# A graph layer on one core: more gathered rows moved to the sync engine and ScalarE, layers spread over three blocks, counts and merges on VectorE

## The chip, the core and the metric

The kernel runs on one core of a Trainium2 chip. The metric is device time in microseconds, the median of several runs. The core has TensorE (PE in the profile: matrix products, weights loaded by PEld), VectorE (DVE), ScalarE (ACT), GpSimd (POOL) and the sync engine (SP). DMAs are issued by SP, ScalarE and GpSimd.

## What is computed

There are 12,500 nodes with 128 features in `x`, and 200,000 edges from `src` to `dst`, sorted by `dst`. The reference, cut to what matters:

```
h    = max(layernorm(x), 0)                  # 12500 x 128
agg  = segment_sum(h[src], dst) / max(deg, 1)
h0   = relu(agg @ Wg + h @ Ws + bg)          # 128 wide
h1   = tanh(h0 @ W1 + b1)                    # 512 wide
h2   = tanh(h1 @ W2 + b2)                    # 512 wide
out  = x + h2 @ W3 + b3                      # 128 wide
```

`deg` counts the edges of each `dst`.

## The kernel before, in words

**Edges.** The 200,000 edges are cut into 1563 chunks of 128. For a chunk, 128 rows of `h` (512 bytes each) must be fetched, one for each `src`, into a 128 x 128 tile. A one-hot matrix of 128 edges by a window of nodes (144 in most chunks, since `dst` is sorted) says to which node each edge belongs. One product of TensorE with the rows as weights (`add`, L432) adds the chunk's rows into the sums of a block of nodes. There are 28 blocks, 23 of 512 nodes and smaller ones at the end.

**Where rows come from.** First the layer norm is computed and written to a table in HBM (`htab`, L173 to L246). Most chunks fetch their rows with one indirect DMA on GpSimd (`gather`, L308). The tiles of these are a ring of `AHEAD` = 32 buffers, so the gather of a chunk can be issued when the chunk 32 places earlier has been added. 80 "raw" chunks (256 to 655, 8 of each 40) are gathered straight from `x` while the table is still being made (L149) and normed on VectorE (`centre`, `raw_scaled`), with the squares on ScalarE. 38 "slow" chunks use no gather: each of their 128 rows is one plain DMA of 512 bytes whose address is read into a register. SP issues them for 23 chunks (tile `srows`), ScalarE for 15 (tile `arows`), in `row_loads` (L337). `SLOW0`, `EACH` and `EACH_A` choose these chunks: one on SP after each 58 gathered chunks, one on ScalarE after each 76. `row_loads` is a generator; the main loop resumes it at a pace that loads a chunk while `EACH` (or `EACH_A`) gathered chunks go by. 32 row addresses are read by one register load before their 32 DMAs. SP's generator stops after each 32 rows, ScalarE's after each 4. `rows_one` has two buffers for each of the two names.

**Order on the queues.** PE, ACT and SP instructions of the main part are kept in program order each (`pe`, `act`, `sp_dma`). On SP the row loads share the queue with three large DMAs for each block: own rows of `htab` (`hb`, L480, one buffer, issued 52 chunks and turned 10 chunks before its block begins), rows of `x` (`xb`), and the store of the output. On ScalarE they share it with the activations of the layers. Each DMA of SP and ScalarE signals its landing on one of eight semaphores, handed out in turn over both queues in the order in which the scheduler places the DMAs. A DMA that takes a semaphore waits until the semaphore's last DMA has landed, whichever of the two engines issued that one.

**Counts.** For each group of 8 chunks VectorE makes the one-hot matrices (`onehot`, L374, four buffers) and sums them over the chunks (`cnt`). `count` (L404) adds these on TensorE by products with a matrix of ones, some ten for each block, and takes the reciprocal on VectorE (`rd`).

**Edges of blocks.** A chunk whose window reaches two blocks goes to an extra sum (`edge`), which ScalarE copies to SBUF (`sums`, two buffers). `merge` (L463) adds it to both blocks by products with the identity. `part0` then multiplies by `rd` (L533).

**Layers.** `layers` (L599) gives the steps of a block: `part0` (h0), `part1` (h1), `part2` (h2), `part3` and `part4` (output, turned back by TensorE, residual added). A block takes the last two parts of the block before between its own, so layers of two blocks overlap. One step is taken for every second chunk until chunk `QUICK` = 1376. After that a plan of expected landing times in the loop (L669) places the steps.

Of the kernel before, what the change touches and what calls it, by code (L numbers as in the profile page):

```python
# [22 lines left out]
F32 = mybir.dt.float32  # L23
BF16 = mybir.dt.bfloat16
# [7 lines left out]
P = 128  # L32
# [7 lines left out]
STEP = 40  # L40
AHEAD = 32
SLOW0 = 120
EACH = 58
EACH_A = 76
TOGETHER = 4
LOADS = 32
LATE = 12
LEAD = 10
QUICK = 1376

# [10 lines left out]
def windowed(ctx, tc, x, src, dst, Wg, Ws, bg, W1, b1, W2, b2, W3, b3, out, flag):  # L61
# [26 lines left out]
    for c in range(SLOW0, NCH - 12):  # L88
        if raw(c):
            continue  # L90
        if ns <= 0:
            slow_s.append(c)
            ns = EACH
        elif na <= 0 and c < QUICK:
            slow_a.append(c)
            na = EACH_A
        else:
            ns -= 1
            na -= 1
# [22 lines left out]
    raws = ctx.enter_context(tc.tile_pool(name="raws", bufs=1))  # L122
    rows_one = ctx.enter_context(tc.tile_pool(name="rows_one", bufs=2))
    rows_in = ctx.enter_context(tc.tile_pool(name="rows_in", bufs=AHEAD))
# [56 lines left out]

    def centre(pool, xt, k, stats):
        nc.vector.tensor_reduce(stats[:, 0], xt, AX.X, ALU.add)
        nc.vector.scalar_tensor_tensor(xt, spread(stats[:, 0], k), -1.0 / D, xt, op0=ALU.mult, op1=ALU.add)
        sq = pool.tile([P, k, D], F32, name=f"sq{k}")
        nc.scalar.activation(sq, xt, AF.Square)
        nc.vector.tensor_reduce(stats[:, 1], sq, AX.X, ALU.add)
# [114 lines left out]
    def flat(t):  # L302
        return t.rearrange("p a b -> p (a b)")

    def sp_dma(*a):
        tc.keep_in_program_order(nc.sync.dma_start(*a))  # L306

# [17 lines left out]
    class act:  # L325
# [8 lines left out]
        def dma(*a):  # L334
            tc.keep_in_program_order(nc.scalar.dma_start(*a))  # L335

# [32 lines left out]
    for t in oh_bufs:  # L369
        nc.vector.memset(t, 0.0)  # L370

    counts = {}

    def onehot(g):  # L374
        k = min(GRP, NCH - g * GRP)
        lo, w = window(g * GRP)
        is_raw = raw(g * GRP)
        oh = ed.tile([P, GRP, W_RAW], F32, name="ohr", bufs=2) if is_raw else oh_bufs[g % OHS]
        if not is_raw and w < oh_w[g % OHS]:
            nc.vector.memset(oh[:, :, w : oh_w[g % OHS]], 0.0)  # L380
            oh_w[g % OHS] = w
        nc.vector.tensor_tensor(  # L382
            oh[:, :k, :w], lane[:, None, :w].to_broadcast([P, k, w]),
            dloc[:, g * GRP : g * GRP + k][:, :, None].to_broadcast([P, k, w]), op=ALU.is_equal,
        )
        ohs[g] = oh
        step, n = (oh.shape[2], w) if is_raw else (PITCH - per, w + per * (k - 1))
        cnt = ed.tile([P, PITCH], BF16, name="cnt", bufs=16)
        part, row, col = oh.ap
        shifted = bass.AP(tensor=oh.tensor, offset=oh.offset, ap=[part, [col[0], n], [step * col[0], k]])  # L390
        with nc.allow_low_precision(reason="whole numbers up to the chunks of a group"):
            nc.vector.tensor_reduce(cnt[:, :n], shifted, AX.X, ALU.add)  # L392
        counts[g] = (lo, n, cnt)

# [9 lines left out]
    def count(b):  # L404

        n, m = blocks[b]
        dg = flat(ps_m.tile([P, 4, P], F32, name="pm"))
        groups = sorted({c // GRP for c in reach[b]})
        for g in groups:
            lo, w, cnt = counts[g]  # L410
            a0, a1 = max(lo, n), min(lo + w, n + m)
            pe.matmul(
                dg[:, a0 - n : a1 - n], ones, cnt[:, a0 - lo : a1 - lo], start=(g == groups[0]), stop=(g == groups[-1]),
                skip_group_check=True,
            )
        rd = ml.tile([P, BLK], F32, name="rd", bufs=3)
        nc.vector.tensor_scalar(rd[:, :m], dg[:, :m], 1.0, None, op0=ALU.max)  # L417
        nc.vector.tensor_reduce(total[:, b : b + 1], dg[:1, :m], AX.X, ALU.add)
        nc.vector.reciprocal(rd[:, :m], rd[:, :m])  # L419
        rds[b] = rd  # L420
# [11 lines left out]
    def add(c):  # L432
# [4 lines left out]
        if c in across[b]:  # L437
# [7 lines left out]
            if c == across[b][-1]:  # L445
                sums = ed.tile([P, BLK], F32, name="sums", bufs=2)
                act.copy(sums[:, : e1 - e0], edge.pop(b)[:, : e1 - e0])
                edges[b] = sums
# [5 lines left out]
        else:  # L454
            start = False
        pe.matmul(
            acc[b][:, a0 - n : a1 - n], rows, oh[:, a0 - lo : a1 - lo], start=start,
            stop=(c == inside[b][-1] and not across[b]), skip_group_check=True,
        )

    edges = {}

    def merge(b):  # L463

        e0, e1 = edge_span(b)
        sums = edges.pop(b)
        for i in (b, b + 1):
            n, m = blocks[i]
            a0, a1 = max(e0, n), min(e1, n + m)
            new = i not in acc  # L470
            if new:
                acc[i] = ps_a.tile([P, BLK], F32, name="agg")
            pe.matmul(
                acc[i][:, a0 - n : a1 - n], ident, sums[:, a0 - e0 : a1 - e0], start=new, stop=(i == b),
                skip_group_check=True,
            )

    owns, hTs, xss, stores = {}, {}, {}, []

    def own(s):  # L480

        n0 = s * BLK
        n = min(BLK, N - n0)
        k = -(-n // P)
        hb = ml.tile([P, BLK // P, D], F32, name="hb", bufs=1)
        sp_dma(hb[:, :k], htab[n0 : n0 + k * P, :].rearrange("(t p) d -> p t d", p=P))
        owns[s] = hb

    def own_turned(s):
# [4 lines left out]
        for t in range(k):  # L494
            pe.transpose(pt[:, t, :], hb[:, t, :], ident)
        hT = ml.tile([P, BLK], F32, name="hT")
        act.copy(hT[:, : k * P], pt[:, :k, :].rearrange("p t n -> p (t n)"))
# [17 lines left out]

    h0s, h1s, h2s, h3s = {}, {}, {}, {}

# [4 lines left out]
    def wide(b):  # L522

        return (P, 2) if blocks[b][1] <= P else (BLK, 1)

    def part0(b):
        n, mm, hop = costs(b)
        s, off = divmod(blocks[b][0], BLK)
        if n == BLK:
            own_part(b)  # L530
        yield 0, 0
        mT = ml.tile([P, BLK], F32, name="mT")
        nc.vector.tensor_tensor(mT[:, :n], acc[b][:, :n], rds.pop(b)[:, :n], op=ALU.mult)  # L533
        yield mm, 0
        p0 = flat(ps_m.tile([P, 4, P], F32, name="pm"))
        pe.matmul(p0[:, :n], ws, hTs[s][:, off : off + n], start=True, stop=False)
        yield mm, n / 90
        pe.matmul(p0[:, :n], wg, mT[:, :n], start=False, stop=True)
        h0s[b] = ml.tile([P, BLK], F32, name="h0")
# [14 lines left out]
    def part2(b):  # L554
        n, mm, hop = costs(b)
        size, bufs = wide(b)
        h1, h2s[b] = h1s.pop(b), ml.tile([P, HM, size], F32, name=f"h2_{size}", bufs=bufs)
        for m in range(HM):
# [39 lines left out]

    def layers(b, before):  # L599


        part = lambda f, *a: lambda: f(*a)
        last = [] if before is None else [part(part3, before), part(part4, before)]
        if reach[b][-1] + LEAD < QUICK:
            return one_by_one(
                part(part0, b), *last[:1], part(part1, b, True), *last[1:], part(part2, b)
            )
        return one_by_one(
            *last, part(part0, b), part(part1, b, False), part(part2, b), part(part3, b), part(part4, b)
        )  # L610

    order = [c for c in range(NCH) if not raw(c) and c not in slow]
    loading = row_loads(slow_s, mybir.EngineType.SP, sp_dma, "srows", LOADS)
    loading_a = row_loads(slow_a, mybir.EngineType.Activation, act.dma, "arows", TOGETHER)
# [21 lines left out]

    own(0)
    own_turned(0)
    onehot(0)
    onehot(1)  # L640
    counted = 0
    for c in range(NCH):
# [3 lines left out]
        if c % GRP == 0 and g + 2 < ngrp:  # L646
# [3 lines left out]
            if 2 <= g < 2 + NRAW:  # L650
                centre(ed, raw_rows[g - 2], GRP, raw_stats(g - 2))
            if g == 2 + NRAW:
                factors(stats_raw)

        while c % GRP == GRP // 2 and counted < len(blocks) and reach[counted][-1] // GRP <= g + 1:
            count(counted)
            counted += 1
# [3 lines left out]
        if not raw(c) and c not in slow:  # L661
            behind += 1
            batch = behind * P // (EACH * LOADS)
            if behind > SLOW0 - 2 * EACH and batch > (behind - 1) * P // (EACH * LOADS):
                next(loading, 0)
# [12 lines left out]
        if done < len(blocks) and (c - lead if across[done] else c) >= reach[done][-1]:  # L678
            if across[done]:
                merge(done)  # L680
            quick = reach[done][-1] + LEAD >= QUICK

            before = done - 1 if done and reach[done - 1][-1] + LEAD < QUICK else None
            work.append([layers(done, before), 0, 0, 0, quick and blocks[done][1] <= P])
            done += 1
        if (c // span + 1) * BLK < N:
            if c % span == span - 52:
                own(c // span + 1)
            if c % span == span - 10:
                own_turned(c // span + 1)  # L690
        if c < QUICK:
# [385 lines left out]
```

## Time and profile before

| what | value |
|---|---|
| median of 3 runs | 1932.92 us (1929.8 to 1933.98) |
| profiled execution: time, span | 1931.2 us, 1928.7 us |
| busy: POOL, PE, DVE, ACT | 1442.0, 1299.0, 1066.8, 228.1 us |
| instructions in it: POOL, PE, DVE, ACT | 1533, 5212, 651, 362 |
| row loads of SP and of ScalarE | 2944 and 1920, 0.5 KB each |
| granted TensorE clock | 0.866 of full speed |
| DMA | 139.69 MB, mean 72 GB/s |

The span runs from the first to the last instruction; 2.5 us of the execution's own time lie outside it. Busy times of different engines overlap. PE counts two records for each float32 product. Issuing a DMA counts as busy on POOL alone, not on SP or ACT; the timeline shows their issues as SPq and ACTq.

### The profile page before, as it was taken

The page shows a single profiled execution, that of the slowest core. Times are in us where ns is not written, and L with a number is a line of the kernel's source. Part 1 is how long each engine was busy: PE and PEld are TensorE (multiplying, and loading weights), DVE is VectorE, ACT ScalarE, POOL GpSimd, SP SyncE. Part 2 cuts the span into 40 slices and gives each one's busy share as a digit, 9 for nine tenths or more (in the row PEclk, how much of TensorE's full clock was granted, in tenths as well). Part 3 has the DMA queues.
Part 4 walks back from the last instruction along what each step waited for, and adds up shares of the span by engine and source line. Part 5 has one row for each costly group of instructions (what it writes and reads, how often), then busy time and mean ns, then how long its engine had stood idle before and what let it go on. Part 6 is the DMA issues. An engine that isn't in the chain of part 4 may idle for free.

```text
span 1928.7 us, 24991 instructions
## 1 busy us (share of the span) xinstructions
PE 1299.0 (67%) x5212; PEld 819.1 (42%) x5212; DVE 1066.8 (55%) x651; ACT 228.1 (12%) x362; POOL 1442.0 (75%) x1533
## 2 busy tenths in 40 slices
PE   0056487775757678758775676566776746878787
PEld 0034354443535445534443344344443424554466
DVE  7964865555556856636544465354554536645430
ACT  1100111010101111111100110001101101101122
POOL 7777777777777777777777777777777777777774
PEclk9999688898878888888887898878988879879698
DMA  8822222222222222222222222222222222222221
GB/s 202 233 65 53 55 67 59 61 71 60 67 71 66 66 70 67 71 71 61 65 61 66 71 61 65 61 71 66 61 66 66 61 70 61 71 78 71 66 62 40
DMA packets 128692, 139.69 MB, mean 72 GB/s; under 512 B 35036, under 2 KB 103294, under 8 KB 128336
## 3 DMA queue, kind: packets, MB, share of 16 engines
q0 software_dynamic: 48800, 100.04, 20.5%
q1 hardware_dynamic: 72654, 33.65, 6.4%
q10 hardware_dynamic: 7076, 4.32, 0.9%
q14 instruction: 119, 0.97, 0.2%
q8 instruction: 43, 0.70, 0.2%
HBM read 125.07 MB, written 12.82 MB: 71 GB/s over the span
## 4 chain that ended last, share of the span: by engine, by line
DMA 31%; PE 28%; issue 17%; SPq 11%; DVE 5%; POOL 3%; ACTq 3%; ACT 1%; POOLq 0%; DVEq 0%
PE pm L297 16%; DMA rows<-htab,scol 16%; SPq L306 10%; PE agg L297 6%; DMA arows<-htab 5%; PE edge L297 4%; DMA srows<-htab 4%; POOL rows L310 3%; DMA hb<-htab 3%; ACTq L335 3%; DVE cnt L392 2%; DMA xt<-in_x_dram 2%; PE pt L300 1%; DVE oh L382 1%; SPq L344 1%
## 5 line engine op out<-in xcount | busy, mean ns | idle before, releaser
L310 POOL DMA_INDIRECT rows<-htab,scol x1445 | 1363.4, 944 | 440.8 <-issue 258.9
L297 PE MATMUL pm<-h,w 128*128 128x512 f32 (+4 forms) x1344 | 649.1, 580 | 26.3 <-ACT h L329 26.3
L297 PE MATMUL agg<-oh,rows 128*128 128x144 f32 (+3 forms) x2068 | 484.4, 342 | 219.9 <-DMA rows<-htab,scol 217.1
L297 PEld LDWEIGHTS agg<-oh,rows 128*128 128x128 f32 x2068 | 360.7, 215 | 530.1 <-DMA rows<-htab,scol 395.2
L382 DVE TENSOR_TENSOR oh<-shared,dloc 128x1152 f32<-128x1152 f32 (+2 forms) x186 | 243.4, 1314 | 605.8 <-PE edge L297 354.9
L392 DVE TENSOR_REDUCE cnt<-oh 128x200 bf16<-128x1600 f32 (+2 forms) x186 | 525.8, 2832 | 5.4
L297 PEld LDWEIGHTS pm<-h,w 128*128 128x128 f32 x1344 | 223.4, 206 | 42.2 <-ACT h L329 29.4
L297 PEld LDWEIGHTS edge<-oh,rows 128*128 128x128 f32 x822 | 150.3, 219 | 160.5 <-issue 85.8
L297 PE MATMUL edge<-oh,rows 128*128 128x144 f32 (+2 forms) x822 | 181.8, 333 | 39.7 <-DMA rows<-htab,scol 39.4
L300 PE MATMUL pt<-ident,hb 128*128 128x128 f32 x98 | 24.5, 398 | 242.7 <-DMA hb<-htab 242.7
L329 ACT ACTIVATE h<-pm,b2c 128x512 f32<-128x512 f32 (+4 forms) x112 | 70.8, 632 | 447.6 <-PE pm L297 229.3
L300 PEld LDWEIGHTS pt<-ident,hb 128*128 128x128 f32 x98 | 16.8, 204 | 246.3 <-issue 246.3
L153 POOL DMA_INDIRECT raw<-in_x_dram,rsrc x80 | 77.7, 971 | 25.4 <-issue 23.8
L329 ACT ACTIVATE h<-pm,b1c 128x512 f32<-128x512 f32 (+4 forms) x112 | 69.9, 632 | 203.2 <-PE pm L297 107.3
L419 DVE RECIPROCAL rd<-rd 128x512 f32<-128x512 f32 (+4 forms) x28 | 81.8, 2920 | 0.0
L332 ACT COPY hT<-pt 128x512 f32<-128x512 f32 (+1 forms) x25 | 14.4, 577 | 410.2 <-PE pt L300 383.9
L589 DVE TENSOR_TENSOR o<-pt,xb 128x512 f32<-128x512 f32 x23 | 15.8, 688 | 75.9 <-PE pt L300 75.9
L417 DVE TENSOR_SCALAR rd<-pm 128x512 f32<-128x512 f32 (+4 forms) x28 | 17.2, 616 | 63.1 <-PE pm L297 63.1
L212 PE MATMUL pm<-ident,idx_f 98*128 98x98 f32 x32 | 6.2, 376 | 62.0 <-DVE idx_f L208 55.7
L297 PE MATMUL pm<-mT,wg 128*128 128x512 f32 (+4 forms) x56 | 32.6, 669 | 22.7 <-DVE mT L533 22.5
L329 ACT ACTIVATE h<-pm,bgc 128x512 f32<-128x512 f32 (+4 forms) x28 | 17.7, 632 | 240.0 <-PE pm L297 144.1
L297 PE MATMUL pm<-hT,ws 128*128 128x512 f32 (+4 forms) x56 | 34.8, 711 | 0.0
(72 smaller groups left out, 496.9 us busy)
## 6 DMA issues: line engine op xcount, KB each, us to landing
srows<-htab SPq DMA_DIRECT2D x2944, 0.5 KB
arows<-htab ACTq DMA_DIRECT2D x1920, 0.5 KB
rows<-htab,scol POOLq DMA_INDIRECT x1445
hb<-htab SPq DMA_DIRECT2D x24, 256.0 KB
xb<-in_x_dram SPq DMA_DIRECT2D x23, 256.0 KB
out_dram<-o SPq DMA_DIRECT2D x23, 256.0 KB
htab<-h SPq DMA_DIRECT2D x6, 896.0 KB
xt<-in_x_dram SPq DMA_DIRECT2D x5, 896.0 KB
```

The source lines that it names most:

```text
L153: nc.gpsimd.indirect_dma_start(out=t[:, j, :], out_offset=None, in_=x, in_offset=bass.IndirectOffsetOnAxis(ap=rsrc[:, g, j : j + 1], axis=0),)
L297: tc.keep_in_program_order(nc.tensor.matmul(*a, **k))
L300: tc.keep_in_program_order(nc.tensor.transpose(*a, **k))
L306: tc.keep_in_program_order(nc.sync.dma_start(*a))
L310: nc.gpsimd.indirect_dma_start(out=r, out_offset=None, in_=htab, in_offset=bass.IndirectOffsetOnAxis(ap=scol[:, c : c + 1], axis=0),)
L329: tc.keep_in_program_order(nc.scalar.activation(*a, **k))
L335: tc.keep_in_program_order(nc.scalar.dma_start(*a))
L344: loads, vs = nc.values_load_multi_w_load_instructions(place[i : i + 1, p0 : p0 + LOADS], engines=[engine], min_val=0, max_val=(N - 1) * ROWB,
L382: nc.vector.tensor_tensor(oh[:, :k, :w], lane[:, None, :w].to_broadcast([P, k, w]), dloc[:, g * GRP : g * GRP + k][:, :, None].to_broadcas ...
L392: nc.vector.tensor_reduce(cnt[:, :n], shifted, AX.X, ALU.add)
L417: nc.vector.tensor_scalar(rd[:, :m], dg[:, :m], 1.0, None, op0=ALU.max)
L419: nc.vector.reciprocal(rd[:, :m], rd[:, :m])
```

## The change

- The constants give 27 slow chunks to SP (one after each 50 gathered chunks) and 20 to ScalarE (one after each 62, now up to chunk 1438). 1436 chunks are gathered, where 1445 were.
- SP's generator stops after each 4 rows instead of 32. `rows_one` has 4 buffers a name, the gathers' ring 44.
- `in_turn` ties each row load, block load and store of SP and ScalarE to the one before it in program order, over both engines, for the scheduler alone: no wait on the chip comes with it. The eight semaphores are so handed out in program order.
- Each group's counts are added on VectorE to a bfloat16 tile of the block (`deg`). One product with ones remains for a block.
- `merged` replaces `merge`: VectorE adds the block's own sums and the one or two edge sums stretch by stretch, and multiplies by `rd`. It is a step of its own (`mean`).
- The squares of the raw chunks move from ScalarE to VectorE.
- Layers: until `QUICK` (now 1312), the steps of a block are its mean, output part 3 of the block two before, its `part0`, `part2` of the block before, `part4` of the block two before, and its `part1`. `LEAD`, the distance at which a block's steps start, is 16 chunks instead of 10.
- `hb` has two buffers; it is loaded half-way through the block two before its own and turned half-way through the block before. `hT` has 3 buffers, `sums` 4 (288 wide).
- `xb` is loaded in `part2` instead of `part0`.

The diff, cut to its core:

```diff
-AHEAD = 32
-SLOW0 = 120
-EACH = 58
-EACH_A = 76
+AHEAD = 44
+SLOW0 = 110
+EACH = 50
+EACH_A = 62
...
-LEAD = 10
-QUICK = 1376
+LEAD = 16
+QUICK = 1312
...
-        elif na <= 0 and c < QUICK:
+        elif na <= 0 and c < NCH - 2 * EACH_A:
...
-    rows_one = ctx.enter_context(tc.tile_pool(name="rows_one", bufs=2))
+    rows_one = ctx.enter_context(tc.tile_pool(name="rows_one", bufs=4))
...
-        sq = pool.tile([P, k, D], F32, name=f"sq{k}")
-        nc.scalar.activation(sq, xt, AF.Square)
+        sq = pool.tile([P, k, D], F32, name=f"sq{k}", bufs=bufs)
+        if bufs > 1:
+            nc.scalar.activation(sq, xt, AF.Square)
+        else:
+            nc.vector.tensor_tensor(sq, xt, xt, op=ALU.mult)
...
+    turn = []
+
+    def in_turn(start):
+
+        tc.keep_in_program_order(start)
+        if turn:
+            tc.add_manual_dep(
+                start.ins, turn.pop(),
+                mybir.DependencyInfo(mybir.DependencyClass.NoSync, mybir.DependencyReason.DATA), reason="in_turn",
+            )
+        turn.append(start.ins.name)
+
     def sp_dma(*a):
-        tc.keep_in_program_order(nc.sync.dma_start(*a))
+        in_turn(nc.sync.dma_start(*a))
...
         def dma(*a):
-            tc.keep_in_program_order(nc.scalar.dma_start(*a))
+            in_turn(nc.scalar.dma_start(*a))
...
-        counts[g] = (lo, n, cnt)
+            for b, (n0, m) in enumerate(blocks):
+                a0, a1 = max(lo, n0), min(lo + n, n0 + m)
+                if a0 < a1:
...
+                    d = counts[b][:, a0 - n0 : a1 - n0]
+                    nc.vector.tensor_tensor(d, d, cnt[:, a0 - lo : a1 - lo], op=ALU.add)
...
+        pe.matmul(dg[:, :m], ones, counts.pop(b)[:, :m], start=True, stop=True)
...
+    def merged(b, mT):
...
+        cuts = sorted({a for a0, a1, _, _ in parts for a in (a0, a1)})
+        for a0, a1 in zip(cuts, cuts[1:]):
+            over = [t[:, a0 - o : a1 - o] for p0, p1, t, o in parts if p0 <= a0 and a1 <= p1]
+            out = mT[:, a0 - n : a1 - n]
+            s = over[0]
+            for t in over[1:]:
+                nc.vector.tensor_tensor(out, s, t, op=ALU.add)
+                s = out
+            nc.vector.tensor_tensor(out, s, rd[:, a0 - n : a1 - n], op=ALU.mult)
...
-        hb = ml.tile([P, BLK // P, D], F32, name="hb", bufs=1)
+        hb = ml.tile([P, BLK // P, D], F32, name="hb", bufs=2)
...
+        if c % span == span // 2 and (c // span + 1) * BLK < N:
+            own_turned(c // span + 1)
+            if (c // span + 2) * BLK < N:
+                own(c // span + 2)
...
-                part(part0, b), *last[:1], part(part1, b, True), *last[1:], part(part2, b)
+                part(mean, b), *of(older, part3), part(part0, b), *of(prev, part2), *of(older, part4),
+                part(part1, b, True),
...
-    loading = row_loads(slow_s, mybir.EngineType.SP, sp_dma, "srows", LOADS)
+    loading = row_loads(slow_s, mybir.EngineType.SP, sp_dma, "srows", TOGETHER)
```

## The prediction

> **What bounds the kernel now.** I read the page's groups first, then POOL's own timeline and its busy time by stretch, then what PE and SP wait for, and last the timeline of SP's queue.
>
> ```profile
> L310 POOL DMA_INDIRECT rows<-htab,scol x1445 | 1363.4, 944 | 440.8 <-issue 258.9
> ```
>
> ```profile
> 88.74 0.94 POOL L153 DMA_INDIRECT raw<-in_x_dram,rsrc  x1 [0.30 <-issue]
> 89.98 0.94 POOL L153 DMA_INDIRECT raw<-in_x_dram,rsrc  x1 [0.30 <-issue]
> ```
>
> ```profile
> 200.00:300.00 100.00, 75.58 (x81) 0.72 0.24 60
> ...
> 1800.00:1900.00 100.00, 75.63 (x81) 0.91 0.23 59
> ```
>
> A gather takes 0.94 us, the next starts 0.30 us later, and every stretch of 100 us from 200 to 1900 holds 80 or 81 of them. The last starts at 1908.0, the first at 105.0: (1908.0 - 105.0) / 1444 = 1.2486 us each, the pitch of two neighbours with nothing waiting between them. POOL never stops, from the raw gathers to the end. The page's 75% is a full engine: the other quarter is the 0.30 us. DMA is at 0.23 to 0.29 of its engines, so bytes don't bind. The end stands 20.7 us behind the last gather (1928.7 - 1908.0): landing, last adds, the last block's layers, its store.
>
> ```profile
> PE pt L300 <- DMA hb<-htab: 242.7, 19, 31.4
> PE agg L297 <- DMA rows<-htab,scol: 217.1, 338, 6.8
> PE pm L297 <- ACT h L329: 26.3, 12, 12.4
> ```
>
> ```profile
> SPq L306 <- DMA arows<-htab: 397.1, 270, 40.0
> ```
>
> PE waits for gathered rows, as it should, and up to 31 us at a time for a block's own rows (`hb`), which queue on SP behind row loads. None of it reaches POOL: the tightest ring buffer came free 3.0 us before its gather (near 600 us, PE's adds set beside the gathers in order). SP waits most for ScalarE's row loads, whose semaphores it shares.
>
> **What the change removes.** Nine gathers: 9 x 1.2486 = 11.2 us, all on the path. Last gather: 105.0 + 1435 x 1.2486 = 1896.8. The start is covered: the nine more address loads sit on ScalarE before and between the last norm pieces; `hb`, which waits for the whole table, issues at 96.6, so 8.4 us are spare before the gather at 105.0.
>
> PE loses the 294 products for counts (23.8 us) and 108 records of merges (21.3 us), and gets 28 wide products (an estimate: 0.4 us each, from 0.27 for 200 columns). Worth nothing at the end, since PE waits 217 us for rows already; it helps PE catch up.
>
> **What it adds on VectorE.** The changed program has 294 count adds, 28 clears, 188 operations in `merged` instead of 28 multiplies, and 10 squares. From 0.25 us (the 128-wide add) for small ones and 1.2 us (a 1024-wide raw operation) for squares: 294 x 0.25 + 28 x 0.2 + 188 x 0.28 - 28 x 0.65 + 12 = 126 us, from 1067 to about 1190, 62% of the span. Tightest are groups 2 to 11, each of 8 x 1.25 = 10 us: 7.9 us now, then 7.9 + 1.2 + 2 x 0.25 = 9.6. One-hots are made two groups ahead, so 20 us cover this. Taken at 0; without that cover PE would start each group late. In the tail the last block's mean takes three operations instead of one: +0.4 us.
>
> Here a rule speaks against the change. The Trainium skill, "SBUF — State Buffer", section "Who interferes with whom", says that a VectorE instruction with two SBUF inputs contends with a GpSimd instruction that reads SBUF, each blocking the other whole, though not with one that only writes. The kernel before keeps one input in PSUM nearly everywhere; count adds, squares and the multiplies by `rd` after a merge now have both in SBUF. The gather names an index column in SBUF, so by the rule some 420 x 0.25 + 12 = 117 us could block gathers, three quarters of it (0.94 of 1.25) on top of one: +88 us. The trace has one such operation:
>
> ```profile
> 89.17 0.23 DVE L261 SCALAR_TENSOR_TENSOR dloc<-rdst,low 128x80 f32<-128x80 int32 x1
> ```
>
> It lies wholly inside the gather of 88.74, which took 0.94 as ever; all 1445 table gathers took 0.940 to 0.961 us. By the row it costs 0. I take the row and keep 88 us as the end of the cost.
>
> **What it moves: the two row-load queues.** SP must load 128 rows in 50 x 1.2486 = 62.4 us instead of 72.4, ScalarE in 77.4 instead of 94.9. In the changed program's order 2407 of SP's 3456 row loads wait for SP's own load four before (650 of 2944 now), 753 for one of ScalarE's (797 now). Such a wait ends 1.5 us after the earlier load's issue, the median by the semaphores' records, so about 0.38 us a row.
>
> ```profile
> 900.40 12.21 SPq L306 DMA_DIRECT2D srows<-htab  x32
> ...
> 958.38 41.50 SPq L306 DMA_DIRECT2D srows<-htab  x64
> 999.98 0.41 SPq L306 DMA_DIRECT2D out_dram<-o  x1
> 1003.24 25.29 SPq L306 DMA_DIRECT2D srows<-htab  x64
> ```
>
> ```profile
> 1642.06 36.43 SPq L306 DMA_DIRECT2D srows<-htab  x96
> ```
>
> The last line is SP alone: (36.43 - 2 x 2.8) / 3 = 10.3 us for 32 rows, 2.8 us being the gap of a register load. Beside ScalarE, 32 rows take 12.2 to 13.1 where nothing else stops them (12.7), and far more where SP waits for ScalarE. Flowing, a chunk needs 4 x 12.7 + 4 x 2.8 + 2.5 large DMAs x 0.45 = 63.1 us, against 62.4: a loss of 0.7 a chunk, 18 us over 26 chunks. A second rule would say worse: "DMA: Bandwidth & Descriptors", section "Anatomy of one DMA", puts a DMA's fixed part at about 2.0 us (for GpSimd's path). With four in flight that is 0.5 us a row, 76 us a chunk, and the loads could not keep up. The measured 1.5 us on these queues decides.
>
> The loss has cover. By the order and the waits of the changed program, the last row of an SP chunk depends on PE only up to 66 or more adds before its use (11 at the tightest now), ScalarE's 28 or more (27 now), and `hb` 66 or more after the start-up (10 now). 66 adds are about 79 us at 1.2 us each. Behind that, the ring of 44 lets PE be 44 x 1.2486 = 55 us late before POOL stops. ScalarE: 16 rows take 6.5 us, so 128 take 52; four register loads at 2.8 and 10 activations at 0.66 make 70 of 77.4 us. Queued behind a late row load on ScalarE are activations, and PE's layer products wait for these with three PSUM tiles of cover; PE waits 26 us for them now. With layers over three blocks most activations have other work between them and their reader. On SP `hb`, `xb` and stores stand behind row loads; only `hb` can hold PE, and its 242.7 us should nearly go. What is late next is again gathered rows. I take 0 for the queues.
>
> **Sum.** 1928.7 - 11.2 + 0.4 = 1917.9 us span; with the 2.5 us around it (1931.2 - 1928.7) 1920.4. The median stood 1.7 above that execution: 1922.1.
>
> **Rivals.**
>
> *The queues become the bound.* ScalarE waits in order for PE, SP for ScalarE's semaphores, and the stalls stay. The two lines from 958 to 1028.5 show 70.2 us for 128 rows. Against 62.4 that is 7.8 lost a chunk, 203 over 26; 79 and 55 are absorbed, 69 are stalled gathers: 1991. It decides from (79 + 55) / 26 = 5.2 us lost, 67.6 us a chunk, and 63.1 is not far below. For it: the 397 us, and ScalarE's lead barely grows. Against it: a good part of that stall is a ring (PE held by `hb`, ScalarE by PE, SP by ScalarE) that the earlier `hb` opens, and eight semaphores in program order let neither queue wait for a load placed later. Chance 0.18.
>
> *VectorE blocks the gathers*, up to 1922 + 88 = 2010, as costed. One overlapping row is thin evidence. Chance 0.05.
>
> *A short stall eats the gain*: PE or ScalarE is once over 55 us late, most likely in the raw part, where PE has 25% more chunks a gather, and 4 to 15 us of gathers are lost: 1926 to 1937. Chance 0.09.
>
> *The change doesn't do what it says*: excluded for counts, since the changed program holds exactly 1436 gathers, 3456 and 2560 row loads, and its landing waits follow program order.
>
> **Chances and range.** The forecast has 0.68, with its own range 1919 to 1927: POOL's chain leaves nothing to gain beyond it, and start and tail may move by a few us. About 0.2% (3.9 us) is what a measurement of this kernel can tell from no change. Faster 0.68, same 0.08 (most of the short stall), slower 0.24 (the queues, VectorE, the rest). The range goes to 1950, which takes in the short stall and mild forms of the queues' case and leaves out some 0.18 above and 0.02 below.
>
> **What would show it.** Right: 1436 gathers at 1.25 us with no gap over 0.31, the last near 1897; `hb` gone from PE's waits; SP's 128 rows under 67 us; VectorE near 1190 us. Wrong: gathers that wait for PE's adds, with PE waiting for `srows`, `arows` or activations (the queues), or gathers longer than 0.96 us (VectorE).

## The result: slower, and the profile after

The changed kernel takes 1981.57 us (1974.13 to 1983.79), the kernel before beside it 1933.45 (1929.8 to 1934.18): a ratio of 1.0246, 95% interval 1.0216 to 1.0276. Forecast was 1922.1. The profiled execution has a span of 1981.9 us, and the gathers themselves are as forecast (the page's groups, columns as before):

```profile
L325 POOL DMA_INDIRECT rows<-htab,scol x1436 | 1364.1, 950 | 488.1 <-issue 247.1
```

There are 1436 of them, the first at 104.1, and POOL's idle time grew from 440.8 to 488.1 us though nine gathers are gone. POOL's busy time by stretch shows where (busy us, gathers, granted clock, DMA share, GB/s):

```profile
200.00:300.00 100.00, 64.77 (x66) 0.67 0.18 46
300.00:400.00 100.00, 72.84 (x77) 0.76 0.23 61
...
1200.00:1300.00 100.00, 75.55 (x81) 0.81 0.24 66
...
1600.00:1700.00 100.00, 59.91 (x64) 0.78 0.24 64
1700.00:1800.00 100.00, 71.62 (x76) 0.80 0.23 62
```

For over 1200 us in the middle POOL is as full as before. The loss lies around 300 and around 1700. Summed over the gathers' starts in the trace: nine gathers less, -11.2 us; an earlier start, -0.9; starts further apart than 1.2486 us, +59.3 (stalls of 18.8 near 300, 4.4 near 690, 20.9 near 1700 and 5.1 near 1790; some 6 of lengthened gathers; some 4 of a pitch of 1.252 instead of 1.249); and a longer tail, +6.1 (the tail is the time behind the last gather: that is at 1955.1, and 26.9 us follow, where 20.7 did). Together 53.3; the spans differ by 53.2.

**The first stall, read backwards.** POOL's timeline, then PE's, then ScalarE's (start, duration, instruction, in brackets the idle time before it and what ended it):

```profile
303.57 0.94 POOL L325 DMA_INDIRECT rows<-htab,scol  x1 [18.97 <-PE agg L300]
```

```profile
275.28 2.08 PE L300 MATMUL pm<-mT,wg 128*128 128x512 f32 x2 [47.10 <-DVE mT L501]
...
300.74 2.08 PE L300 MATMUL pm<-h,w 128*128 128x512 f32 x2 [21.58 <-ACT h L344]
```

```profile
249.00 0.30 ACT L193 ACTIVATE shared<-shared,eps 128x80 f32<-128x80 f32 x1 [99.21 <-DVE oh L398]
249.07 25.05 ACTq L350 DMA_DIRECT2D arows<-htab  x48
274.16 0.39 ACT L347 COPY sums<-edge 128x280 f32<-128x280 f32 x1 [24.86 <-DMA srows<-htab]
274.25 25.71 ACTq L350 DMA_DIRECT2D arows<-htab  x48
300.00 0.69 ACT L344 ACTIVATE h<-pm,bgc 128x512 f32<-128x512 f32 x1 [25.45 <-DMA arows<-htab]
```

At 249.00 ScalarE computes a square root for the statistics of all raw chunks (`factors`, L193). VectorE releases it only then, and since the scheduler put it behind no more than 4 row loads, everything later on ScalarE has waited 99 us for it. 48 row loads follow, and behind them the copy of `sums` at 274.16; VectorE's `mT` waits for that copy, PE for `mT` (47.10). 48 more loads, and only then the activation that PE waits for next (21.58). That is 68.7 us of idle time in which PE adds almost nothing, with a ring of 44 x 1.2486 = 55 us before POOL stops; PE is 74 us behind the gathers at the worst. SP is held too, by ScalarE's landing semaphores. Three lines of waits answer to those shown of before (us in total, times, longest):

```profile
SPq L321 <- DMA arows<-htab: 135.5, 66, 96.2
```

```profile
PE pt L303 <- DMA hb<-htab: 33.3, 1, 33.3
```

```profile
PE pm L300 <- ACT h L344: 499.6, 115, 25.1
```

**Between the events.** PE's wait for activations, the last of these lines, was 26.3 us before. 392 of the 499.6 us fall between 400 and 1600, where PE waits for no row: it is late, so its rows have landed, and what holds it is activations that stand behind row loads. Followed back from the last instruction, the chain of what each step waited for runs for 75% of that stretch through SP's row loads (landings 47.7%, issues 15.1%, register loads 12.5%), for 7.1% through the landings of ScalarE's. So SP's queue sets the pace there and reaches PE by way of ScalarE. POOL loses little by it while the ring lasts, but PE can't catch up.

**The second.** PE's timeline, then ScalarE's, then POOL's:

```profile
1677.63 5.93 PE L300 MATMUL pm<-h,w 128*128 128x512 f32 x8 [3.10 <-ACT h L344]
1685.39 10.57 PE L300 MATMUL pm<-h,w 128*128 128x512 f32 x24 [1.83 <-ACT h L344]
...
1754.10 2.08 PE L300 MATMUL pm<-h,w 128*128 128x512 f32 x2 [25.05 <-ACT h L344]
```

```profile
1700.62 46.44 ACTq L350 DMA_DIRECT2D arows<-htab  x80
1747.16 0.39 ACT L347 COPY sums<-edge 128x280 f32<-128x280 f32 x1 [46.02 <-DMA arows<-htab]
```

```profile
1700.35 0.94 POOL L325 DMA_INDIRECT rows<-htab,scol  x1 [21.20 <-PE agg L300]
```

When the loop reaches chunk 1312 (`QUICK`), all pending layer steps are issued at once (the burst, below): from 1671.3 to 1699.7 PE multiplies for the layers and adds no chunk, and activations that it waits for stand behind row loads. From 400 us on PE had been 39 to 48 us late (medians of 75 chunks each, an add's start less its gather's), so 10 to 16 us of the ring were left for these 28 us: POOL stops for 21. Then 80 row loads stand before the copy of `sums`, PE waits 25.05 for the activation behind it, and POOL loses 5 more.

### The profile page after: what moved, and what is told of

The parts are those of the page before. It is cut to its first block, busy times and chain, and to the rows that moved or that the text cites. A ratio compares the mean times of both kernels' runs of the same rounds, so it can differ in the third digit from the quotient of the medians.

```text
span 1981.9 us, 27036 instructions
## 1 busy us (share of the span) xinstructions
PE 1213.4 (61%) x4838; PEld 800.4 (40%) x4838; DVE 1155.0 (58%) x1143; ACT 217.3 (11%) x352; POOL 1441.9 (73%) x1524
## 4 chain that ended last, share of the span: by engine, by line
DMA 48%; SPq 21%; PE 10%; issue 7%; DVE 6%; ACTq 5%; POOL 2%; ACT 1%; DVEq 0%; POOLq 0%
DMA srows<-htab 36%; SPq L321 11%; SPq L359 9%; PE pm L300 7%; DMA arows<-htab 6%; ACTq L359 3%; ACTq L350 3%; POOL rows L325 2%; DMA rows<-htab,scol 2%; PE agg L300 2%; DMA xt<-in_x_dram 2%; DVE cnt L408 1%; ACT h L344 1%; DVE oh L398 1%; DMA xb<-in_x_dram 1%
## 5 line engine op out<-in xcount | busy, mean ns | idle before, releaser
L325 POOL DMA_INDIRECT rows<-htab,scol x1436 | 1364.1, 950 | 488.1 <-issue 247.1
L300 PE MATMUL pm<-h,w 128*128 128x512 f32 (+4 forms) x1344 | 698.4, 619 | 409.9 <-ACT h L344 394.4
L300 PEld LDWEIGHTS agg<-oh,rows 128*128 128x128 f32 x2046 | 383.2, 231 | 376.3 <-issue 305.7
L300 PE MATMUL agg<-oh,rows 128*128 128x144 f32 (+3 forms) x2046 | 418.1, 335 | 40.4 <-DMA rows<-htab,scol 34.7
L300 PEld LDWEIGHTS pm<-h,w 128*128 128x128 f32 x1344 | 230.0, 213 | 457.5 <-ACT h L344 421.6
L300 PEld LDWEIGHTS edge<-oh,rows 128*128 128x128 f32 x826 | 135.5, 201 | 99.4 <-issue 79.6
L499 DVE TENSOR_TENSOR mT<-agg,sums 128x136 f32<-128x136 f32 (+6 forms) x57 | 15.2, 271 | 268.7 <-PE agg L300 204.9
L300 PE MATMUL edge<-oh,rows 128*128 128x144 f32 (+2 forms) x826 | 147.3, 301 | 7.2 <-DMA rows<-htab,scol 7.2
L300 PE MATMUL pm<-deg,ones 128*128 128x512 bf16 (+1 forms) x24 | 12.1, 504 | 99.9 <-ACT h L344 95.9
L418 DVE TENSOR_TENSOR deg<-deg,cnt 128x200 bf16<-128x200 bf16 (+5 forms) x279 | 54.7, 223 | 3.8
L300 PEld LDWEIGHTS pm<-mT,wg 128*128 128x128 f32 x56 | 10.3, 222 | 86.4 <-DVE mT L501 85.6
```

The lines of the kernel that those rows point to most:

```text
L300: tc.keep_in_program_order(nc.tensor.matmul(*a, **k))
L325: nc.gpsimd.indirect_dma_start(out=r, out_offset=None, in_=htab, in_offset=bass.IndirectOffsetOnAxis(ap=scol[:, c : c + 1], axis=0),)
L418: nc.vector.tensor_tensor(d, d, cnt[:, a0 - lo : a1 - lo], op=ALU.add)
```

## The experiments

Theory: two single events on ScalarE's queue, whose instructions stay in order, costly because queues that must load a chunk in 62.4 us have no rate left to make up for lateness. In the recorded expectations this is Q. Rivals: the queues are overloaded all along (O); VectorE's two-input operations block gathers (V). "Both mends" below are the first two edits together.

### The square root in its place

```diff
-                factors(stats_raw)
+                act.activation(stats_raw[:, 1], stats_raw[:, 1], AF.Sqrt, bias=eps, scale=1.0 / D)
+                nc.vector.reciprocal(stats_raw[:, 1], stats_raw[:, 1])
```

Through `act` the square root keeps its place in program order, behind 100 row loads instead of 4.

> One edit to the changed kernel: the square root of the raw chunks' statistics on ScalarE keeps its place in program order, behind 100 of ScalarE's row loads instead of behind 4. Theory Q (two single events on ScalarE's queue: row loads stuck 99 us behind that square root, and a burst of 80 row loads ahead of a copy at the switch of the layer plan): the stall of 18.8 us of gathers near 300 us goes, the one of 21 us near 1700 us stays, about 1962 us. Theory O (both queues are loaded beyond what they can carry all along, PE 42 us late throughout, so the same loss appears later): within 5 us of the changed kernel's 1982 us. Theory V (VectorE blocks gathers): within 5 us of 1982 us as well.

1936.24 us, ratio 1.0039 (1.0024 to 1.0053): one instruction moved, and by the ratios 40 us are gone ((1.0246 - 1.0039) x 1933), more than the event's own 19 and twice what Q had said, since Q took the two events as independent. The stretches of POOL:

```profile
200.00:300.00 100.00, 76.19 (x79) 0.84 0.21 56
...
1600.00:1700.00 100.00, 74.76 (x80) 0.81 0.26 69
1700.00:1800.00 100.00, 72.32 (x78) 0.87 0.26 71
```

The second stall has nearly gone too, though nothing was changed there. PE's lateness is 3 us near 300 and grows only from 10 near 400 to 23 near 1500, and the ring absorbs most of the same burst. So the events are linked: the lateness of the first lasts to the second. O, which expects stalls all along, falls.

### No row loads of ScalarE past chunk 1312

```diff
-        elif na <= 0 and c < NCH - 2 * EACH_A:
+        elif na <= 0 and c < QUICK:
```

> One edit to the changed kernel: ScalarE loads no chunk after chunk 1312 (the rule of the kernel before), so 18 chunks instead of 20 and 1438 gathers. Theory Q: the stalls near 1700 and 1780 us (26 us) go, and most of the 6 us by which the tail is longer; two more gathers cost 2.5 us: about 1953 us, with the stall near 300 us still there. Theory O: about 1980 us, the stalls move elsewhere. Theory V: 1984 us.

1955.94 us, ratio 1.0155 (1.0126 to 1.0184), with 1438 gathers. The stall near 300 stays (the stretch from 200 to 300 has 66 gathers, as in the changed kernel); the burst now stops POOL for 3.7 us instead of 20.9, since its activations no longer stand behind row loads (the activations from the first `b1c` of the burst to its `hT` copy take 30.5 us, 39.5 before), and the tail is 20.4 us.

### Both

> Both edits of the two runs beside it on the changed kernel, the pace of 50 and 62 kept: 1438 gathers. Theory Q: hardly any stalled gather is left (under 6 us), 1930 to 1937 us, although PE still runs some 40 us late in the middle. Theory O: over 1960 us. Theory V: over 1970 us.

1925.64 us, ratio 0.9978 (0.9971 to 0.9985): faster than both kernels, and by more than expected. POOL's stretches:

```profile
200.00:300.00 100.00, 76.22 (x79) 0.85 0.21 56
...
1600.00:1700.00 100.00, 75.59 (x81) 0.89 0.27 71
```

No stall is left but 2.9 us of lengthened gathers between 200 and 250. Seven gathers fewer than before are 8.7 us; the last is at 1903.0, where it was 1908.0. The granted clock doesn't explain the loss: it was 0.821 in the changed kernel's profile and 0.866 before, but 0.843 here, in a kernel that is faster than both.

### The squares back on ScalarE

```diff
-        if bufs > 1:
+        if bufs > 0:
```

> One edit to the changed kernel: the squares of the raw chunks run on ScalarE again, where the scheduler puts all ten and the square root ahead of every row load. Theory Q: the row loads stay stuck until about 250 us, so the stall near 300 us stays at 15 to 25 us, and only the nine gathers that the squares lengthened (4 us in all) are back at 0.95 us: 1976 to 1982 us. Theory V: if squares and gathers collide for more than the records show, 1960 us or less. A theory that VectorE's extra work in the first 250 us is what makes the rows late: the stall goes, about 1960 us.

1983.29 us, ratio 1.0270 (1.0253 to 1.0287). The scheduler puts the squares and the root ahead of every row load, and the event stays (ScalarE's timeline):

```profile
246.02 0.30 ACT L193 ACTIVATE shared<-shared,eps 128x80 f32<-128x80 f32 x1 [2.76 <-DVE oh L398]
248.39 52.31 ACTq L350 DMA_DIRECT2D arows<-htab  x100
```

No gather is longer than 1.165 us here, and the time is about the same (Q had said 1976 to 1982): V is not the cause, nor is it that the squares moved to VectorE.

### Four runs where the kernel before took 2613.7 us

These four ran on a chip on which the kernel before took 2613.69 us (2600.17 to 2626.5, at a granted clock near 0.756), so their ratios can't be set beside the others.

The pace alone undone (first edit), the pace alone done (second, in the kernel before), both mends without the tie of the two queues in `in_turn` (third), and both mends with the raw squares on ScalarE in program order (fourth). The three constants are written on one line here:

```diff
-SLOW0 = 110, EACH = 50, EACH_A = 62
+SLOW0 = 120, EACH = 58, EACH_A = 76
...
-SLOW0 = 120, EACH = 58, EACH_A = 76
+SLOW0 = 110, EACH = 50, EACH_A = 62
...
-        if turn:
+        if False:
...
-            nc.vector.tensor_tensor(sq, xt, xt, op=ALU.mult)
+            act.activation(sq, xt, AF.Square)
```

> All of the change is kept but the three numbers that choose the slow chunks, which go back to the kernel before's (120, 58, 76; 1445 or a few fewer gathers). The Sqrt still stands early in ScalarE's queue and ScalarE's row loads still reach past chunk 1312. Theory Q (two single head-of-line events, which cost what they do because the queues at 62.4 us a chunk have no spare rate to catch up with): at 72.5 us a chunk SP catches up 8 to 10 us with every chunk, so the first event (some 19 us of stalled gathers near 300 us) stays in part, the later lateness falls to under 25 us, and the second event is mostly absorbed by the ring: 1940 to 1955, against 1981.6 with the new pace. If the events cost the same whatever the pace: 1975 to 1992. If the pace alone was the fault and the events nothing: 1928 to 1934.

> The kernel before with only the three numbers of the new pace (110, 50, 62; with its own limit for ScalarE's chunks; counts, layers, semaphores, ring of 32 and squares as before). If the rest of the change is what makes the pace possible: SP has 62.4 us for a chunk that took it up to 70.2 in the trace of before, 26 times up to 7.8 is 203 us, of which the ring of 32 (40 us) and the lead absorb at most 120: 1960 to 2020, PE late on srows for most of the run. If the faster pace would have worked without the rest (SP's waits in before are mere slack that closes up): 1920 to 1930.

> The changed kernel with both mends (Sqrt at its place in program order, no slow chunks of ScalarE past chunk 1312; 1925.6 us) but without the tie that hands out the eight landing semaphores in program order: they go out in the order in which the scheduler places the DMAs. If that order matters, loads wait for loads of the other engine that are placed later in its queue: SP over 65 us a chunk, PE's lateness past the ring's 55 us, 1940 to 1985. If it doesn't: 1922 to 1930. Theory Q says nothing on it; I lean to the first, since SP waits for ScalarE's loads in before (397 us) far more than in the changed kernel.

> The changed kernel with both mends, and the ten squares of the raw chunks back on ScalarE at their own places in program order (not ahead of the row loads, as they came to stand when they were left to the scheduler). Expected: the few gathers that two-input VectorE operations lengthen near 200 to 250 us go (2.9 us in the run with both mends), no stall comes in their place, 1922 to 1924. If ScalarE's queue has no room for ten operations of 0.9 us among its first row loads: stalls near 300 us and 1930 or more. If squares on VectorE cost nothing: 1925.6 again.

Ratios: 0.971 (0.9663 to 0.9757), 1.0602 (1.0549 to 1.0655), 1.0627 (1.0575 to 1.0678), 1.0099 (1.0064 to 1.0134). In the fourth kernel, one of POOL's stretches and one line of SP's timeline show what is different:

```profile
800.00:900.00 100.00, 49.41 (x53) 0.76 0.18 47
```

```profile
894.72 25.82 SPq L321 DMA_DIRECT2D srows<-htab  x32
```

A gather still takes 945 ns, but 32 row loads take a median of 20.6 us (13.2 in the same kernel's later run, below), SP's 128 rows 89.2 us (63.2), and PE's weight loads for `agg` wait 547 us for no cause that the trace shows (289). It is the issue itself: of the 3456 register moves that stand before SP's row loads and wait for nothing, 454 take over 0.5 us, 324 us in all, against none in the later run; the median is 29 ns in both. Row loads are many instructions; where issue is slow, the queues bind at either pace, and a faster pace loses. Why issue is slow there stays open. The four kernels were run again beside a kernel before of 1933.39 us.

### The old pace in the changed kernel

> The changed kernel with the three numbers of the old pace (120, 58, 76), once more, since in its first run the kernel before itself took 2613.7 us, with every engine's instructions issued more slowly; there this kernel was 0.971 of before. At the usual 1930 us of the kernel before: theory Q (two single events, costly because queues at 62.4 us a chunk have no spare rate) expects 1938 to 1955, since at 72.5 us SP catches up 8 to 10 us with every chunk: the first event stays, PE's lateness falls to under 25 us between the events and the second is mostly absorbed by the ring. If the events cost the same at any pace: 1975 to 1992. If the pace alone was the fault: 1928 to 1934.

1942.24 us, ratio 1.0051 (1.0034 to 1.0067). Both events are still in the program (the square root stands behind 12 row loads and waits 98.4 us), and cost one stall (POOL's timeline):

```profile
290.44 0.94 POOL L325 DMA_INDIRECT rows<-htab,scol  x1 [6.73 <-PE agg L300]
```

PE's lateness then falls, by medians of 75 gathers, from 29.8 to 19.4, 13.7, 3.8 and 3.1 us, 6 to 10 us in each 94 us, and the burst near 1610 raises it to 23: absorbed. In the changed kernel the same medians are 42.5, 31.1 (just behind the stall), 39.5, 42.4, 47.9. SP needs 61 to 65 us for a chunk while it catches up in this run, so at 72.4 us it has 7 to 11 to spare and at 62.4 hardly any. PE's wait for activations is 60.9 us in all here, where it was 499.6 in the changed kernel (and 401.8 with both mends, at the new pace). This is the direct evidence for the missing reserve.

### The new pace in the kernel before

> The kernel before with the three numbers of the new pace (110, 50, 62) alone, once more, for the same reason; at the slower issue it was 1.060 of before. At 1930 us: if the rest of the change is what makes the pace possible, SP needs up to 70.2 us for a chunk that must be there in 62.4, and 1960 to 2020 follows, with PE late on srows for most of the run. If its waits are only slack that closes up under the faster pace: 1920 to 1930.

1982.40 us, ratio 1.0255 (1.0238 to 1.0272). SP takes a median of 66.8 us for 128 rows, and POOL stalls by 2 to 9 us a dozen times from 560 to 1580 us. PE's wait for a block's rows is there as before the change:

```profile
PE pt L300 <- DMA hb<-htab: 362.2, 20, 25.6
```

### Both mends without the tie

> The changed kernel with both mends but without the tie that hands out the landing semaphores in program order, once more; at the slower issue it was 1.063 of before, and the kernel with the tie (and squares on ScalarE) 1.010. At 1930 us: if the order of the semaphores matters, loads wait for loads of the other engine that stand later, SP takes over 65 us a chunk, and 1940 to 1985 follows; if it doesn't, 1922 to 1930. The first is the likelier after the slower runs.

1977.44 us, ratio 1.0223 (1.0206 to 1.0240), against 0.9978 with the tie. The waits of PE, then POOL's stretches:

```profile
PE pt L303 <- DMA hb<-htab: 293.2, 18, 31.0
...
PE agg L300 <- DMA srows<-htab: 96.7, 9, 25.3
```

```profile
1600.00:1700.00 100.00, 69.46 (x74) 0.83 0.24 64
```

SP's chunk takes 66.0 us instead of 63.2, and small stalls from 740 to 1700 us add up to 40 us. This is what O had described, and the tie prevents it: the semaphores in program order are worth 2.4% at the new pace. It also shows that two buffers and the earlier load don't remove the wait for `hb` by themselves. At 1.0223 this kernel is near the kernel before at the new pace (1.0255), which points to the tie for most of what makes the pace possible. The tie alone in the kernel before wasn't run, nor counts, merges or layers each alone.

### Both mends, squares on ScalarE in program order

> The changed kernel with both mends and the ten raw squares on ScalarE at their own places in program order, once more; at the slower issue it was 1.010 of before. At 1930 us: the gathers that two-input VectorE operations lengthen near 200 to 250 us go (2.9 us in the run with both mends) and no stall comes in their place: 1922 to 1924. If ScalarE's queue has no room for ten operations of 1.06 us among its first row loads: 1930 or more. If squares on VectorE cost nothing: 1925.6 again.

1926.59 us, ratio 0.9961 (0.9949 to 0.9974), the lowest ratio of all, though its interval overlaps that with the squares on VectorE (0.9971 to 0.9985): which of the two is faster is not settled. The stretch from 200 to 300 holds 81 gathers again, none of them over 1.02 us, and ScalarE had room for the ten squares.

### The tie alone taken away

> The changed kernel without the tie between the two queues, nothing else. In this program the scheduler puts the Sqrt behind 100 row loads of ScalarE instead of 4, with no other edit: so if the tie is what set the Sqrt ahead of them, the stall near 300 us is gone here (POOL runs 80 or 81 gathers from 200 to 400 us), though the squares are still on VectorE. What replaces it: landing semaphores out of program order, as in the kernel with both mends and no tie (1977 us, 46 us of small stalls from 740 to 1700 us), and ScalarE's late row loads, whose burst near 1700 us then meets a ring that is already used up: 5 to 20 us more. 1978 to 2000. If the moved squares were the cause of the first stall instead, it stays, and 1995 to 2015 follows.

2014.96 us, ratio 1.0449 (1.0432 to 1.0467), above the 2000 expected. In this program 100 row loads stand before the square root, as ScalarE's timeline has it, and POOL's stretches show no stall there (78 gathers and not 81 in the first, since gathers under squares are longer):

```profile
151.68 23.30 ACTq L350 DMA_DIRECT2D arows<-htab  x52
...
198.75 23.68 ACTq L350 DMA_DIRECT2D arows<-htab  x48
...
248.55 0.30 ACT L193 ACTIVATE shared<-shared,eps 128x80 f32<-128x80 f32 x1 [18.94 <-DVE oh L398]
```

```profile
200.00:300.00 100.00, 76.49 (x78) 0.74 0.20 53
300.00:400.00 100.00, 75.59 (x81) 0.85 0.24 63
```

So the tie, not the moved squares, put the root ahead. A likely reason is that the tie binds the row loads to each other in the scheduler, so that an instruction outside that order slips in front of them; how the scheduler came to it isn't shown. Why this kernel lost still more is read from its starts: small stalls of 42 us from 740 to 1650, then 27 us from 1700 on, and a tail of 34.9 us. The other reading named a like time (1995 to 2015), but with the stall near 300, which isn't there.

## Why the prediction was wrong, point by point

- **POOL bounds, 1.2486 us a gather, nine gathers worth 11.2 us:** right. The pitch is 1.252 in the median, and where nothing stalls 80 or 81 start in 100 us.
- **SP's chunk at 63.1 us against 62.4, a loss of 0.7:** right, with some luck: 32 rows take a median of 13.1 us (12.7 forecast), the gap of a register load is 2.3 (2.8). The median chunk is 63.7, in the kernel with both mends 63.2, and PE's lateness there grows to some 20 us, near the 18 that were summed. The rule of the Trainium skill, "DMA: Bandwidth & Descriptors", "Anatomy of one DMA", would have given an estimate of 76 us a chunk from 2.0 us for a DMA's fixed part; a row load of SP lands 1.6 us after its issue here.
- **"I take 0 for the queues":** the step that failed. It compared rates and leads, and asked of each queue whether it keeps up. It named what stands behind a late row load on ScalarE (activations, with PE's layer products waiting for them) and dismissed it with "most activations have other work between them and their reader"; that wait of PE went from 26 to 499.6 us. It didn't read the changed program's order on ScalarE for one instruction that waits long, with what is queued behind it: a root with 99.21 us to wait, and 96 row loads between it and the activation that PE needs. Together with the burst at `QUICK`, which the prediction didn't look at, this is 45 of the 64 us by which the span missed (18.8 + 20.9 + 5.1). The rest is mostly lengthened gathers and pitch (some 10), the tail (5.7) and the small stall near 690 (4.4).
- **The same step, the cover.** "PE be 44 x 1.2486 = 55 us late before POOL stops" is right, but was counted as if each event found it full. At a loss of 0.7 a chunk nothing refills it. The square root mended alone saved 40 us, 19 of them at the event itself.
- **"Taken at 0" for VectorE's additions:** the busy time is 1155.0 us (forecast 1190), and the one-hots had their cover. That the last raw sums on VectorE would end a wait on ScalarE was missed.
- **Contention:** between the ends, near the row. The Trainium skill, "SBUF — State Buffer", "Who interferes with whom", was weighed at 88 us against 0 by the one overlapping row. Measured: 25 gathers of 1436 are longer than 0.97 us, together 5.9 us; each has a VectorE operation over it that reads both inputs from SBUF. So the traces agree with the rule, but only about the start of a gather (last section). The one row couldn't show that: its operation began 0.43 us into the gather (89.17 - 88.74). POOL's timeline, then VectorE's, for one of the 25:

```profile
217.68 1.64 POOL L325 DMA_INDIRECT rows<-htab,scol  x1 [0.30 <-PE agg L300]
```

```profile
217.35 1.15 DVE L189 TENSOR_TENSOR sq<-raw 128x1024 f32<-128x1024 f32 x1
```

- **Wait for `hb`:** 242.7 to 33.3 us, as forecast, but not by the two buffers and the earlier load: with these and without the tie it is 293.2, with both mends and the tie 30.7.
- **Tail +0.4:** 6.1. In the changed kernel PE is still 11 to 23 us late in the last gathers; in the kernel with both mends it isn't, and the tail is 19.4. But it is 24.9 in the kernel with both mends and the squares on ScalarE, with no lateness, so the whole cause isn't shown.
- **The rival "the queues become the bound", 1991:** near the time by another way. From 400 to 1600 POOL is full but for 4.4 us near 690, which a steady loss of 7.8 us a chunk excludes; that picture is the kernel without the tie. *A short stall eats the gain* was the right kind of case, priced at 4 to 15 us since a stall was thought of as one event, with queues that recover.

## What to carry to other kernels

When a queue is loaded to its rate, read its new order for single instructions that wait long and for what stands behind them, since a queue without spare rate keeps every delay until the next one comes. An order imposed on some instructions moves the others: what isn't bound to it may slip ahead and block it. Spare time in a ring is spent once, so price two events together.

## What the runs showed of the hardware

- A VectorE operation with two SBUF inputs can lengthen a gather when it runs about the gather's start, and hardly when it begins well inside the gather. In the changed kernel ten gathers start under a square of 128 x 1024. Nine become longer, up to 1.81 us from 0.944, and end 0.81 to 0.82 us after the square, as in the lines above (217.68 + 1.64 is 0.82 behind 217.35 + 1.15). The tenth starts only 8 ns before its square ends. Of nine more gathers during which a square started none is longer. The other 16 long gathers lie under short count adds and multiplies. All 25 have such an operation over the point 0.13 us behind their start; 1358 gathers have none there, and the longest of these takes 0.957 us.
- Where instructions issue slowly (the runs beside 2613.7 us), operations keep their durations, 945 ns for a gather, but SP gets through a row load, with all that lies between, in 0.70 us (89.2 / 128) instead of 0.49 (63.2 / 128), as 454 of 3456 register moves take over 0.5 us where all took some 29 ns. The changed kernel at the old pace (4992 row loads) was then 0.971 of before, with both mends at the new pace (5760) 1.010.
